# Two graph layers on one core: h M and h Wv^T by Strassen's scheme, half-size slots for adj and exp(a), interleaved weight loads, more slots for the last results

## The chip, the core and the metric

The kernel runs on one core of a Trainium2 chip, in fp32 throughout. TensorE (PE) multiplies, VectorE (DVE) adds and reduces, ScalarE (ACT) applies functions and copies, GpSimd (POOL) computes one power per tile and issues stores, SyncE (SP) issues loads. The metric is the device time of one execution in microseconds; the runs' median is given beside the one profiled execution.

## The reference

x is 3327 x 512, adj 3327 x 3327 with a full diagonal, all weights 512 x 512:

```python
h = relu(layernorm(x))
q, k, v = h @ Wq.T + bq, h @ Wk.T + bk, h @ Wv.T + bv
a = q @ k.T / sqrt(512) + adj + adj
x = x + softmax(a) @ v
h = relu(layernorm(x))
A2 = adj + I;  d = diag(A2) ** -0.5
temp = A2 @ h @ W.T
x = x + relu((d[:, None] * A2 * d[None, :]) @ temp)
```

## The kernel before

Rows are padded to 3328 = 26 tiles of 128 (`HALF` = 13 tiles each half). Matrix products are cut into 2 x 2 blocks and done by a scheme of seven block products instead of eight (Strassen's in Winograd's form): some sums of blocks are made on DVE first, and results are put together from shared partial results. A matmul's cost on PE depends on the width of its moving operand, 512 at most, one PSUM bank.

Since q k^T = h Wq^T Wk h^T plus terms, the kernel first makes M = Wq^T Wk and the vector u = Wk^T bq; keys are then h itself, and queries are q' = (h M + u) * scale. The stages, in order of program text:

1. **M and u** (L218-237). Wq's four blocks of rows, then Wk's four, then four x tiles and bv are loaded on SP's queue in that order; 16 matmuls make M, 16 narrow ones u.
2. **Layernorm and projections** (L184-296). A tile of x is loaded into one of four slots of `x_ring` (L192), `norm` (L168) takes its statistics on DVE and the power on POOL, ACT applies the relu in place, PE transposes four 128 x 128 pieces, ACT copies them to the block's `hb` and to `hp[t]`. `hp[t]` holds seven combinations of h's 2 x 2 blocks for key tile t, four of them made by DVE adds (L262-265); they are the scores' left operands. A block is 2 to 4 tiles; `h_transposed(b + 1)` stands ahead of `project(b)`. `project` makes q' transposed, four output blocks by four contraction blocks, moving width 512, 384 or 256, stored by POOL to `qd`; then v, four matmuls of width 512 a tile, stored to `vd`.
3. **Scores** (L303-406), 4 groups of query columns (two 448 wide, two 384 wide in each of four quarters) by 13 steps t. For a step, `adjacency` loads four quarter blocks of adj transposed into one slot of `g_ring` (4 slots, L304); `outer_sums` makes the four sums that the graph layer will need (`four_sums`, L149) in one of two `o` slots and stores them; `scores` does seven products of two matmuls. A bank Y is read by `plus` (L358) after each of the products 0-0, 4-5 and 2-7 and then accumulated onto, so that one product's value goes into several results. The last product is put off into the next step (`rest`, L377). ACT takes exp of g's halves (L373, L381/383), and one store writes all of g to `pd` (L384). Half a group ahead, `queries` loads four blocks of q' and `more_queries` makes four differences (L155).
4. **Attention** (L409-519). exp(a) is read back, `values` reads v and makes its differences, seven products a step of width 256, summed over 13 steps in seven banks; `attend` puts the results together in `cx`, divides by the row sums (L488), stores the new x and the new h.
5. **Graph layer** (L548-802). Two rounds g of the same recursion one level deeper: `Step` loads blocks of adj or their stored sums into `a_ring`, makes `four_sums` into `o_ring3`, `Right` makes the right operand's blocks in `b_ring`, `gather` puts the products together in `cts`. `temp` (L713) multiplies by W, `finish` (L723) transposes a result tile back, scales, adds x, and stores it from one of three slots of `out_ring` (L569). The last six half tiles are finished after the last step (L801).

On-chip memory is one `arena` with tags `big`, `half`, `quarter` (L95-102): a new tile under a tag waits until everything that used the tag's last tile is done. The order on each engine is made by a scheduler from the program text; the DMA queues of SP and POOL issue in order, so that an issue that waits for a slot holds those behind it.

Of the kernel before, what the change touches and what calls it, by code (L numbers as in the profile page):

```python
# [44 lines left out]
def graph_layers_kernel(  # L45
# [45 lines left out]

    arena = ctx.enter_context(tc.tile_pool(name="arena", bufs=1))
    banks = ctx.enter_context(tc.tile_pool(name="banks", bufs=1, space=bass.MemoryType.PSUM))

    def big(k, shape, name):  # L95
        return arena.tile(shape, F32, name=name, tag=f"big{k}")
# [44 lines left out]
    qd = [dram.tile([P, DC, 2 * H[s]], F32, name=f"qd{s}") for s in range(2)]  # L141
    vd = [dram.tile([P, D], F32, name=f"vd{i}") for i in range(NT)]
# [41 lines left out]
    hp = [big(t, [P, 7, 2, P], f"hp{t}") for t in range(HALF)]  # L184

    blocks = []
    for s in range(2):
        for a, z in ((0, 4), (4, HT[s])):
            for y in range(2):
                blocks.append((s, [STRIPS[s] + y * HT[s] + k for k in range(a, z)]))  # L190

    x_ring = ring((big, 13), (big, 14), (big, 15), (big, 16))  # L192
    v_ring = ring((big, 17), (big, 18), (quarter, 0))
    hb_ring = ring((half, 4), (half, 5), (half, 8), (half, 9), (half, 2), (half, 3))
    qs_ring = ring((half, 6), (half, 7), (half, 10), (half, 11))
# [4 lines left out]
    mm_ring, tp_ring, av_ring = psum_ring(0, 1, 2, 3), psum_ring(4, 5), psum_ring(6, 7)  # L200

    def load_x(i):
        xt = x_ring([P, D], "xt")
        nc.sync.dma_start(xt, x[i * P : (i + 1) * P])
        return xt

    def weight(name, src, slots):

        parts = []
        for k in range(2):  # L210
            w = half(slots[k], [P, 2, D], name)
            for c in range(2):
                r = (2 * k + c) * P
                nc.sync.dma_start(w[:, c], src[r : r + P])
            parts += [w[:, 0], w[:, 1]]
        return parts

    w_q = weight("wq", wq, (12, 13))  # L218
    w_k = weight("wk", wk, (0, 1))
    first = {i: load_x(i) for i in blocks[0][1]}  # L220
    bv_sb = quarter(1, [P, D], "bv_sb")
    nc.sync.dma_start(bv_sb, bass.AP(tensor=bv.tensor, offset=bv.offset, ap=[[0, P], [1, D]]))
    M = [m[:, c] for m in (half(14, [P, 2, D], "M"), half(15, [P, 2, D], "M")) for c in range(2)]
    u = const.tile([P, DC], F32, name="u")

    ps = [mm_ring("mm") for _ in range(DC)]
    for c in range(DC):
        for r in range(DC):
            nc.tensor.matmul(ps[r], w_q[c][:, r * P : (r + 1) * P], w_k[c], start=c == 0, stop=c == DC - 1)  # L229
    for r in range(DC):  # L230
        nc.scalar.copy(M[r], ps[r])
    pu = tp_ring("pu")
    for r in range(DC):
        for c in range(DC):
            nc.tensor.matmul(pu[:, r : r + 1], w_k[c][:, r * P : (r + 1) * P], bq_sb[:, c : c + 1],
                             start=c == 0, stop=c == DC - 1)
    nc.vector.tensor_copy(u, pu[:, :DC])

    w_v = weight("wv", wvT, (12, 13))

    hT = {}

    def h_transposed(b):

        _, its = blocks[b]
        hb = [hb_ring([P, 2, BW], "hb") for _ in range(2)]
        for k, i in enumerate(its):
            xt = first.pop(i) if i in first else load_x(i)
            rstd, nb = norm(xt)
            nc.scalar.activation(xt, xt, AF.Relu, bias=nb, scale=rstd)  # L250
            pt = tp_ring("tp").rearrange("p (c e) -> p c e", c=DC)
            for c in range(DC):
                nc.tensor.transpose(pt[:, c], xt[:, c * P : (c + 1) * P], ident)  # L253
            own = [a[:, :, k * P : (k + 1) * P] for a in hb]
            for a in range(2):
                nc.scalar.copy(own[a], pt[:, 2 * a : 2 * a + 2])
            t = i % HALF
            if i < HALF:
                nc.scalar.copy(hp[t][:, 0:2], pt.rearrange("p (a c) e -> p a c e", a=2))
            else:  # L260
                nc.scalar.copy(hp[t][:, 2], pt[:, 2:4])
                nc.vector.tensor_add(hp[t][:, 3], own[0], hp[t][:, 2])  # L262
                nc.vector.tensor_add(hp[t][:, 5], own[0], hp[t][:, 0])
                nc.vector.tensor_add(hp[t][:, 4], hp[t][:, 3], hp[t][:, 0])
                nc.vector.tensor_add(hp[t][:, 6], hp[t][:, 1], hp[t][:, 4])
        hT[b] = [hb[c // 2][:, c % 2] for c in range(DC)]

    def project(b):
        s, its = blocks[b]
        wd = len(its) * P  # L270
        hb = hT.pop(b)
        c0 = (its[0] - STRIPS[s]) * P
        for a in range(2):
            qs = qs_ring([P, 2, BW], "qs")
            for o in range(2):
                ps = mm_ring("mm")
                d = 2 * a + o
                for c in range(DC):
                    nc.tensor.matmul(ps[:, :wd], M[c][:, d * P : (d + 1) * P], hb[c][:, :wd],  # L279
# [900 lines left out]
```

## Time and profile before

| | us |
|---|---|
| median of 3 runs | 2306.88 (2306.67 to 2311.48) |
| profiled execution, its own time | 2312.0 |
| its span | 2310.2 |
| PE busy | 2250.0 (97%) |
| DVE busy | 1402.6 (61%) |
| ACT, POOL busy | 221.7, 208.5 |
| M and u, to | 27.1 |
| layernorm and projections, to | 218.6 |
| scores, to about | 757 |
| attention, to | 1276 |
| graph layer, to | 2283 |
| end | 2310.2 |

The profiled execution took 5.1 us more than the median. Shares of busy time are means over stages; a row such as `A <- B: total, times, longest` in the table of waits says how long A's engine stood before A until B was done. A timeline row gives start, length, engine, line, operation, output and inputs, shape, count, and in brackets the idle time before it and what ended it. DMA rows give the time from issue to landing.

### The profile page before, as it was taken

What the parts mean: (1) busy time and instruction counts of PE and PEld (TensorE: products, weight loads), DVE (VectorE), ACT (ScalarE), POOL (GpSimd) and SP (SyncE); (2) the same over time, 40 slices, a digit from 0 to 9 for tenths busy, and PEclk for the clock granted to TensorE, in tenths of its full rate; (3) what the DMA queues carried; (4) which work ended last, traced back from release to release, by engine and by line L of the source; (5) the groups of instructions that cost most, each with busy time, mean ns of one, the idle gap of its engine ahead of it and who ended that gap; (6) DMA issues with size and microseconds to landing.
All of it is one profiled execution on the core that took longest, in us unless ns stands there. A gap on an engine that the chain in (4) does not pass through costs nothing.

```text
span 2310.2 us, 21423 instructions
## 1 busy us (share of the span) xinstructions
PE 2250.0 (97%) x7398; PEld 1379.1 (60%) x7398; DVE 1402.6 (61%) x2845; ACT 221.7 (10%) x336; POOL 208.5 (9%) x332
## 2 busy tenths in 40 slices
PE   8999999999999999999999999999999999999995
PEld 4545444455555788888888555555545455555553
DVE  3344656666556765565655667787645357677773
ACT  3210111121111000000000000000001000000011
POOL 2121111111111010010110100000000000000001
PEclk9999999999999999999999999999999999999998
DMA  4334778777787443444445667766545467666684
GB/s 150 126 123 167 257 260 282 249 265 256 269 278 263 133 150 92 133 138 132 137 135 190 217 211 256 233 208 211 190 147 193 151 211 257 227 200 213 205 273 135
DMA packets 226086, 457.55 MB, mean 198 GB/s; under 512 B 23250, under 2 KB 129072, under 8 KB 225968
## 3 DMA queue, kind: packets, MB, share of 16 engines
q1 hardware_dynamic: 192464, 323.17, 43.8%
q0 software_dynamic: 33504, 132.92, 15.6%
q8 instruction: 60, 0.98, 0.2%
q14 instruction: 58, 0.48, 0.1%
HBM read 323.11 MB, written 132.90 MB: 197 GB/s over the span
## 4 chain that ended last, share of the span: by engine, by line
PE 62%; issue 29%; POOL 4%; DMA 2%; DVE 2%; ACT 0%; SPq 0%; POOLq 0%; DVEq 0%
PE p L660 28%; PE p L516 22%; PE p L718 4%; PE p L652 3%; PE av L287 2%; PE mm L279 2%; POOL sum L346 1%; POOL p L384 1%; PE mm L229 1%; POOL out_dram L88 1%; DMA p<-g 1%; DMA g<-in_adjT_dram 1%; PE tp L253 0%; POOL rstd L177 0%; DVE st L171 0%
## 5 line engine op out<-in xcount | busy, mean ns | idle before, releaser
L660 PE MATMUL p<-o,b 128*128 128x448 f32 (+1 forms) x1344 | 526.8, 514 | 0.0
L660 PE MATMUL p<-a,b 128*128 128x448 f32 (+1 forms) x1008 | 418.1, 513 | 3.7 <-DVE b L623 3.7
L660 PEld LDWEIGHTS p<-o,b 128*128 128x128 f32 x1344 | 255.6, 190 | 213.6 <-issue 120.0
L355 PE MATMUL Y<-qt,hp 128*128 128x448 f32 (+1 forms) x832 | 314.0, 520 | 19.3 <-DVE g L359 19.2
L516 PE MATMUL p<-vr,o 128*128 128x256 f32 x1352 | 322.0, 379 | 2.7 <-DVE vr L157 2.2
L151 DVE TENSOR_TENSOR o<-a 128x896 f32<-128x896 f32 (+1 forms) x168 | 171.8, 1022 | 215.9 <-PE p L660 183.4
L660 PEld LDWEIGHTS p<-a,b 128*128 128x128 f32 x1008 | 189.9, 190 | 161.9 <-issue 91.6
L516 PEld LDWEIGHTS p<-vr,o 128*128 128x128 f32 x1352 | 256.5, 190 | 38.9 <-DVE vr L157 2.6
L355 PEld LDWEIGHTS Y<-qt,hp 128*128 128x128 f32 x832 | 157.1, 191 | 162.0 <-issue 73.3
L516 PE MATMUL p<-vr,pt 128*128 128x256 f32 x1014 | 250.2, 379 | 0.0
L516 PEld LDWEIGHTS p<-vr,pt 128*128 128x128 f32 x1014 | 192.2, 190 | 26.3
L355 PE MATMUL Z<-qt,hp 128*128 128x448 f32 (+1 forms) x416 | 162.4, 513 | 0.0
L509 DVE TENSOR_TENSOR sums<-sums,pt 128x512 f32<-128x512 f32 (+1 forms) x84 | 54.7, 651 | 148.5 <-DMA pt<-p 148.4
L359 DVE SCALAR_TENSOR_TENSOR g<-g,Y 128x448 f32<-128x448 f32 (+1 forms) x156 | 91.1, 584 | 70.0 <-PE Y L355 67.8
L355 PEld LDWEIGHTS Z<-qt,hp 128*128 128x128 f32 x416 | 79.3, 191 | 66.7 <-issue 39.4
L151 DVE TENSOR_TENSOR o<-g 128x896 f32<-128x896 f32 (+1 forms) x52 | 53.2, 1024 | 101.7 <-DMA g<-in_adjT_dram 97.0
L152 DVE TENSOR_TENSOR o<-o,a 128x448 f32<-128x448 f32 (+1 forms) x168 | 98.8, 588 | 3.8
L153 DVE TENSOR_TENSOR o<-o,a 128x448 f32<-128x448 f32 (+1 forms) x168 | 98.8, 588 | 3.4
L718 PE MATMUL p<-w,ct 128*128 128x512 f32 x208 | 93.5, 592 | 0.0
L279 PE MATMUL mm<-hb,M 128*128 128x512 f32 (+2 forms) x256 | 92.0, 512 | 0.0
L287 PE MATMUL av<-wv,hb 128*128 128x512 f32 x208 | 91.2, 593 | 0.0
L652 PE MATMUL p<-a,b 128*128 128x448 f32 (+1 forms) x224 | 82.8, 513 | 0.0
(140 smaller groups left out, 1790.2 us busy)
## 6 DMA issues: line engine op xcount, KB each, us to landing
a<-sum SPq DMA_DIRECT2D x104, 448.0 KB, 5.6
pt<-p SPq DMA_DIRECT2D x78, 512.0 KB, 4.2
a<-sum SPq DMA_DIRECT2D x104, 384.0 KB, 3.7
a<-in_adjT_dram SPq DMA_DIRECT2D x78, 448.0 KB, 4.4
a<-in_adjT_dram SPq DMA_DIRECT2D x78, 384.0 KB, 3.7
g<-in_adjT_dram SPq DMA_DIRECT2D x52, 448.0 KB, 5.7
sum<-o POOLq DMA_DIRECT2D x26, 896.0 KB, 5.5
p<-g POOLq DMA_DIRECT2D x26, 896.0 KB, 4.3
```

Of the source, the lines that this page charges most:

```text
L151: nc.vector.tensor_add(o[:, 0:2], g[:, 0:4:3], g[:, 1:2].to_broadcast([P, 2, g.shape[-1]]))
L152: nc.vector.tensor_add(o[:, 2], o[:, 1], g[:, 0])
L153: nc.vector.tensor_add(o[:, 3], o[:, 2], g[:, 2])
L279: nc.tensor.matmul(ps[:, :wd], M[c][:, d * P : (d + 1) * P], hb[c][:, :wd], start=c == 0, stop=c == DC - 1)
L287: nc.tensor.matmul(ps, hb[c][:, k * P : (k + 1) * P], w_v[c], start=c == 0, stop=c == DC - 1)
L355: nc.tensor.matmul(ps, hp[t][:, a, k], qt[b][:, k], start=start and k == 0, stop=k == 1, skip_group_check=True)
L359: nc.vector.scalar_tensor_tensor(g[:, n], g[:, n], 2.0, ps, op0=ALU.mult, op1=op)
L509: nc.vector.tensor_add(sums, sums, pt[:, 0:2])
L516: nc.tensor.matmul(ps[r][:, m * E : (m + 1) * E], a[:, m * P : (m + 1) * P], vr[t][:, b], start=t == 0 and m == 0, stop=t == HALF - 1, ski ...
L652: nc.tensor.matmul(ps[("p2", "p3", "p4", "p8")[k]][:, :w], b[:, z], a[:, 0, y], start=k == 3, stop=True)
L660: nc.tensor.matmul(ps[r][:, :w], b[:, i], m, start=self.t == 0, stop=self.t == PAIRS - 1 and r in ("p1", "p5", "p6", "p7"))
L718: nc.tensor.matmul(ps, cts[s][d][:, k * P : (k + 1) * P], w1[d], start=d == 0, stop=d == DC - 1)
```

## The change

- **Layernorm and projections.** Tiles are taken in four packs of 3, 3, 3 and 4 tiles from each half, both halves together (6 or 8 tiles). The pack's `hp` holds the seven combinations, and these are now also the left operands of seven-product schemes for q' = h M + u and v = h Wv^T + bv; M and Wv get `four_differences` and a negated first block. `hb` is gone. A class `Chain` holds the order of products and reads that the scores had, and serves q', v and the scores; the last product of a chain is put off into the next chain.
- **Start.** Blocks of Wq and Wk are loaded in turns; the first four x tiles are issued on ACT's queue; Wv has slots of its own and is loaded in halves of a block.
- **Scores.** `g` is split into halves by tile row, with rings of 4 and 5 half-size slots; `o` is split into two of four half-size slots; each half of exp(a) and of the sums is stored by itself, the first half of exp(a) as soon as it is ready.
- **Attention, graph layer.** `cx`, s1, u, v, q and `cts` are smaller tiles; normalization of a tile is done in two halves; the graph layer's rings are views of the packs' space; the first half of the last gather is settled before the last adds of the second.
- **End.** The last six half tiles have six slots for results and six for x.

The diff, cut; where a function is rewritten, only its new lines are given:

```diff
-    def big(k, shape, name):
-        return arena.tile(shape, F32, name=name, tag=f"big{k}")
+    def large(k, shape, name):
+        return arena.tile(shape, F32, name=name, tag=f"large{k}")
+    def mid(k, shape, name):
+        return arena.tile(shape, F32, name=name, tag=f"mid{k}")
...
-    qd = [dram.tile([P, DC, 2 * H[s]], F32, name=f"qd{s}") for s in range(2)]
-    vd = [dram.tile([P, D], F32, name=f"vd{i}") for i in range(NT)]
+    qd = dram.tile([P, DC, NP], F32, name="qd")
+    vd = [dram.tile([P, 4, E], F32, name=f"vd{t}") for t in range(HALF)]
...
+    PACKS = ((0, 3), (3, 3), (6, 3), (9, 4))
+    A = {"m1": 0, "p2": 1, "p4": 2, "p5": 3, "p6": 4, "p7": 5, "p3": 6}
+    B = {"m1": 0, "p2": 2, "p3": 3, "p5": 4, "p6": 5, "p7": 6, "p4": 7}
+    hp = [large(k, [P, 7, 2, n * P], f"hp{k}") for k, (_, n) in enumerate(PACKS)]
+    def h_of(t, product, c):
+        k = next(k for k, (a, n) in enumerate(PACKS) if a <= t < a + n)
+        o = (t - PACKS[k][0]) * P
+        return hp[k][:, A[product], c, o : o + P]
...
+    x_bank, y_bank, z_bank, tp_bank = psum_ring(0, 1), psum_ring(2, 3), psum_ring(4, 5), psum_ring(6, 7)
+    class Chain:
+        before = None
+        def __init__(self, product, first, more, last):
+            X, Y, Z = x_bank("X"), y_bank("Y"), z_bank("Z")
+            product(Y, "m1", True)
+            first(0, Y, -1)
+            product(Z, "p5", True)
+            first(3, Z, -1)
+            product(X, "p2", True)
+            more(0, X)
+            product(Y, "p6", False)
+            first(1, Y, -1)
+            Chain.finish()
+            product(Z, "p3", False)
+            more(1, Z)
+            product(Y, "p7", False)
+            more(3, Y)
+            def rest():
+                product(Y, "p4", False)
+                first(2, Y, 1)
+                last()
+            Chain.before = rest
+        @staticmethod
+        def finish():
+            if Chain.before:
+                Chain.before()
+            Chain.before = None
+    x_ring = ring(*((mid, k) for k in range(4)))
+    v_ring = ring(*((mid, k) for k in range(5, 13)))
+    def load_x(i, queue=nc.sync):
         xt = x_ring([P, D], "xt")
+        queue.dma_start(xt, x[i * P : (i + 1) * P])
...
+    order = [(k, t + y * HALF) for k, (a, n) in enumerate(PACKS) for t in range(a, a + n) for y in range(2)]
+    first = {i: load_x(i, nc.scalar) for _, i in order[:4]}
+    def blocks(slots, name):
+        return [b[:, k] for b in (half(j, [P, 2, 2, E], name) for j in slots) for k in range(2)]
+    w_q, w_k = ([half(k, [P, 2, D], name) for k in slots] for name, slots in (("wq", (0, 1)), ("wk", (2, 3))))
+    for c in range(DC):
+        for w, src in ((w_q, wq), (w_k, wk)):
+            nc.sync.dma_start(w[c // 2][:, c % 2], src[c * P : (c + 1) * P])
+    bv_sb = quarter(0, [P, D], "bv_sb")
     nc.sync.dma_start(bv_sb, bass.AP(tensor=bv.tensor, offset=bv.offset, ap=[[0, P], [1, D]]))
+    w_v = blocks(range(8, 12), "wv")
+    for c in range(DC):
+        for z in range(2):
+            nc.sync.dma_start(w_v[2 * (c // 2) + z][:, c % 2], wvT[c * P : (c + 1) * P, z * E : (z + 1) * E])
+    M = blocks(range(4, 8), "M")
...
+            nc.tensor.matmul(ps[r], w_q[c // 2][:, c % 2, r * P : (r + 1) * P], w_k[c // 2][:, c % 2],
+                             start=c == 0, stop=c == DC - 1)
     for r in range(DC):
+        for z in range(2):
+            nc.scalar.mul(M[2 * (r // 2) + z][:, r % 2], ps[r][:, z * E : (z + 1) * E], scale)
+    pu = bank(4, "pu")
     for r in range(DC):
         for c in range(DC):
+            nc.tensor.matmul(pu[:, r : r + 1], w_k[c // 2][:, c % 2, r * P : (r + 1) * P], bq_sb[:, c : c + 1],
                              start=c == 0, stop=c == DC - 1)
+    nc.vector.tensor_scalar(u, pu[:, :DC], scale, None, op0=ALU.mult)
+    for b in (M, w_v):
+        four_differences(b)
+        nc.scalar.mul(b[0], b[0], -1.0)
...
+    def h_transposed(k):
+        a, n = PACKS[k]
+        for _, i in (o for o in order if o[0] == k):
             xt = first.pop(i) if i in first else load_x(i)
             rstd, nb = norm(xt)
...
+            w = slice((i % HALF - a) * P, (i % HALF - a + 1) * P)
             if i < HALF:
+                nc.scalar.copy(hp[k][:, 0:2, :, w], pt.rearrange("p (a c) e -> p a c e", a=2))
             else:
+                nc.scalar.copy(hp[k][:, 2, :, w], pt[:, 2:4])
+                nc.vector.tensor_add(hp[k][:, 3, :, w], hp[k][:, 2, :, w], pt[:, 0:2])
+                nc.vector.tensor_add(hp[k][:, 5, :, w], hp[k][:, 0, :, w], pt[:, 0:2])
+        nc.vector.tensor_add(hp[k][:, 4], hp[k][:, 3], hp[k][:, 0])
+        nc.vector.tensor_add(hp[k][:, 6], hp[k][:, 1], hp[k][:, 4])
+    def project_q(k):
+        a, n = PACKS[k]
+        w = n * P
+        qs = [half(12 + j, [P, 2, BW], "qs") for j in range(4)]
+        def chain(o):
+            def product(ps, name, start):
+                for c in range(2):
+                    nc.tensor.matmul(ps[:, :w], M[B[name]][:, c, o * P : (o + 1) * P], hp[k][:, A[name], c],
+                                     start=start and c == 0, stop=c == 1, skip_group_check=True)
+            def first(j, ps, sign):
+                d = 2 * (j % 2) + o
+                nc.scalar.activation(qs[j][:, o, :w], ps[:, :w], AF.Identity, bias=u[:, d : d + 1], scale=float(sign))
+            def more(j, ps):
+                nc.vector.tensor_add(qs[j][:, o, :w], qs[j][:, o, :w], ps[:, :w])
+            def last():
+                if o == 1:
+                    for j in range(4):
+                        y, z = divmod(j, 2)
+                        i = (y * HALF + a) * P
+                        nc.gpsimd.dma_start(qd[:, 2 * z : 2 * z + 2, i : i + w], qs[j][:, :, :w])
+            Chain(product, first, more, last)
+        for o in range(2):
+            chain(o)
+    def project_v(k):
+        a, n = PACKS[k]
+        def chain(t0, m):
+            vs = [v_ring([P, 2, E], "vs")[:, :m] for _ in range(4)]
+            def product(ps, name, start):
+                for j in range(m):
+                    for c in range(2):
+                        nc.tensor.matmul(ps[:, j * E : (j + 1) * E], h_of(t0 + j, name, c), w_v[B[name]][:, c],
+                                         start=start and c == 0 and j == 0, stop=c == 1, skip_group_check=True)
+            def of(ps):
+                return ps[:, : m * E].rearrange("p (j e) -> p j e", j=m)
+            def first(j, ps, sign):
+                z = j % 2
+                bias = bv_sb[:, z * E : (z + 1) * E].unsqueeze(1).to_broadcast([P, m, E])
+                (nc.vector.tensor_add if sign > 0 else nc.vector.tensor_sub)(vs[j], bias, of(ps))
+            def more(j, ps):
+                nc.vector.tensor_add(vs[j], vs[j], of(ps))
+            def last():
+                for j in range(m):
+                    for y in range(4):
+                        nc.gpsimd.dma_start(vd[t0 + j][:, y], vs[y][:, j])
+            Chain(product, first, more, last)
+        for t0 in range(a, a + n, 2):
+            chain(t0, min(2, a + n - t0))
...
+        project_q(k)
+        project_v(k)
...
-    g_ring = ring(*((big, k) for k in range(13, 17)))
-    o_ring = ring((big, 17), (big, 18))
-    x_bank, y_bank, z_bank = psum_ring(0, 1), psum_ring(2, 3), psum_ring(4, 5)
+    g_rings = ring(*((mid, k) for k in range(4))), ring(*((mid, k) for k in range(4, 9)))
+    o_ring = ring(*((mid, k) for k in range(9, 13)))
...
-        g = g_ring([P, 4, Q[0]], "g")[:, :, :wd]
+        g = [take([P, 2, Q[0]], f"g{k}")[:, :, :wd] for k, take in enumerate(g_rings)]
         for k in range(2):
             r0, c0 = (k * HALF + t) * P, STRIPS[s] * P
             src = adjT[r0 : r0 + P, c0 : c0 + 2 * H[s]].rearrange("p (y w) -> p y w", y=2)
-            nc.sync.dma_start(g[:, 2 * k : 2 * k + 2], src[:, :, c : c + wd])
+            nc.sync.dma_start(g[k], src[:, :, c : c + wd])
...
-        o = o_ring([P, 4, Q[0]], "o")[:, :, :wd]
-        four_sums(o, g)
+        pair = [o_ring([P, 2, Q[0]], "o")[:, :, :wd] for _ in range(2)]
+        o = [pair[m // 2][:, m % 2] for m in range(4)]
+        nc.vector.tensor_add(o[0], g[0][:, 0], g[0][:, 1])
+        nc.vector.tensor_add(o[1], g[1][:, 1], g[0][:, 1])
+        nc.vector.tensor_add(o[2], o[1], g[0][:, 0])
+        nc.vector.tensor_add(o[3], o[2], g[1][:, 0])
         for n, parts in enumerate(((0, 2, 3), (0, 1, 2, 3), (3,), (1, 2, 3))):
             k, y = divmod(n, 2)
-            d = diagonal(o[:, 0], (k * HALF + t) * P, STRIPS[s] * P + y * H[s] + c)
+            d = diagonal(o[0], (k * HALF + t) * P, STRIPS[s] * P + y * H[s] + c)
             for m in parts if d else ():
-                nc.vector.tensor_add(o[:, m, d[0]], o[:, m, d[0]], d[1])
-        nc.gpsimd.dma_start(sumd[s][t][:, :, c : c + wd], o)
+                nc.vector.tensor_add(o[m][:, d[0]], o[m][:, d[0]], d[1])
+        for m in range(2):
+            nc.gpsimd.dma_start(sumd[s][t][:, 2 * m : 2 * m + 2, c : c + wd], pair[m])
+    def scores(s, q, t, qt, g):
         wd, c = Q[s], q * Q[s]
+        a = [g[0][:, 0], g[0][:, 1], g[1][:, 0], g[1][:, 1]]
+        def product(ps, name, start):
             for k in range(2):
+                nc.tensor.matmul(ps[:, :wd], h_of(t, name, k), qt[B[name]][:, k], start=start and k == 0, stop=k == 1,
                                  skip_group_check=True)
+        def settle(k):
+            if k == 1 and t == HALF - 1:
+                nc.scalar.activation(g[k], g[k], AF.Exp, bias=pad)
             else:
+                nc.scalar.activation(g[k], g[k], AF.Exp)
+            nc.gpsimd.dma_start(pd[s][t][:, 2 * k : 2 * k + 2, c : c + wd], g[k])
+        def first(n, ps, sign):
+            nc.vector.scalar_tensor_tensor(a[n], a[n], 2.0, ps[:, :wd], op0=ALU.mult,
+                                           op1=ALU.add if sign > 0 else ALU.subtract)
+        def more(n, ps):
+            nc.vector.tensor_add(a[n], a[n], ps[:, :wd])
+            if n == 1:
+                settle(0)
+        Chain(product, first, more, lambda: settle(1))
...
-    sum_ring = ring((half, 14), (half, 15))
+    sum_ring = ring((half, 7), (half, 14))
-    b12_ring = ring((big, 15), (big, 16), (big, 17), (big, 18))
+    b12_ring = ring(*((mid, k) for k in range(4, 8)))
...
+        nc.sync.dma_start(vr[t][:, 0], vd[t][:, 0])
+        nc.sync.dma_start(b12, vd[t][:, 1])
+        nc.sync.dma_start(vr[t][:, 1:3], vd[t][:, 2:4])
...
-            nc.vector.scalar_tensor_tensor(xt, cx[y][:, k], rs, xt, op0=ALU.mult, op1=ALU.add)
+            for z in range(2):
+                w = slice(z * E, (z + 1) * E)
+                nc.vector.scalar_tensor_tensor(xt[:, w], cx[y][z][:, k], rs, xt[:, w], op0=ALU.mult, op1=ALU.add)
...
+    def view(k, j):
+        if k not in parts:
+            n = PACKS[k][1]
+            parts[k] = large(k, [P, n, 4, Q[0]], f"part{k}")
+        return parts[k][:, j]
+    def turns(*views):
+        turn = itertools.cycle(views)
+        return lambda: view(*next(turn))
+    a_ring = turns((0, 0), (0, 1), (0, 2), (1, 0), (1, 1))
+    o_ring3 = turns((1, 2), (2, 0), (2, 1))
...
+    spare = ((mid, 10), (mid, 11), (mid, 12))
     ts_ring = ring((quarter, 0), (quarter, 1), (half, 8))
-    xr_ring = ring((quarter, 0), (quarter, 1), (half, 8))
-    out_ring = ring((half, 6), (half, 14), (half, 9))
+    xr_ring = ring((quarter, 0), (quarter, 1), (half, 8), (half, 9))
+    out_ring = ring((half, 6), (half, 7), *spare[:2])
+    xr_last = ring(*((half, k) for k in (15, 14, 10, 11, 8, 9)))
+    out_last = ring((half, 6), (half, 7), *spare, (quarter, 0))
...
+        if r == "p4" and s == 1:
+            settle(lo)
         nc.vector.tensor_add(to[0][:, hi], v, p["p4"])
         nc.vector.tensor_add(to[1][:, hi], to[1][:, hi], p["p8"])
         if r == "p4" and s == 1:
-            settle(lo)
             settle(hi)
...
-        xr = xr_ring([P, D], "xr")
+        xr = (xr_ring if spot is None else xr_last)([P, D], "xr")
-        pt = bank(spot, "pt")
+        pt = bank(ROLE["p8"] if spot is None else spot, "pt")
+            nc.tensor.transpose(pt[:, d * P : (d + 1) * P], cts[s][y][d][:, k * P : (k + 1) * P], ident)
+        o = (out_ring if spot is None else out_last)([P, D], "r")
```

## The prediction

> **What bounds the kernel now.** I read the page's busy shares first (PE 97%, DVE 61%, ACT 10%), then a table of windows cut at the stage borders, because a 97% mean hides where the other 3% and the cheaper work lie.
>
> ```profile
> 7.75:27.10 19.35, 19.35 (x64) 10.41 (x65) 3.96 (x17) 6.77 (x9) 6.69 (x5) 1.00 0.48 139
> 27.10:218.60 191.50, 191.10 (x570) 98.53 (x570) 80.16 (x202) 43.33 (x101) 37.71 (x63) 1.00 0.39 133
> 218.60:495.00 276.40, 269.78 (x713) 134.38 (x712) 176.36 (x321) 48.45 (x51) 36.92 (x52) 1.00 0.74 257
> 495.00:757.70 262.70, 250.05 (x753) 142.74 (x752) 162.34 (x325) 46.77 (x55) 37.01 (x52) 0.99 0.78 268
> 757.70:1276.00 518.30, 515.57 (x2411) 453.40 (x2409) 311.56 (x698) 22.18 (x30) 41.41 (x67) 1.00 0.44 136
> 1276.00:2283.00 1007.00, 1002.06 (x2885) 538.36 (x2884) 662.84 (x1268) 51.67 (x84) 43.95 (x79) 1.00 0.64 212
> 2283.00:2310.20 27.20, 2.10 (x13) 1.24 (x12) 5.03 (x12) 2.52 (x6) 3.98 (x8) 0.60 0.18 61
> ```
>
> Columns: window and length, then PE, weight load, DVE, ACT, POOL, then granted clock, DMA share, GB/s. Rows: M and u; layernorm and projections; the scores' first two and last two groups; attention; the graph layer; the tail. PE is the bound everywhere except the tail; the scores leave it idle for some 19 us, which no other stage does. Next, the PE timeline for what a matmul costs by width (each fp32 matmul is two records; next start minus start, over the count, is the real rate, since ends are modelled):
>
> ```profile
> 74.12 13.90 PE L287 MATMUL av<-wv,hb 128*128 128x512 f32 x32
> 87.86 1.04 PE L253 MATMUL tp<-ident,xt 128*128 128x128 f32 x8
> ...
> 90.46 9.20 PE L279 MATMUL mm<-hb,M 128*128 128x384 f32 x28
> 99.49 5.74 PE L287 MATMUL av<-wv,hb 128*128 128x512 f32 x13
> ...
> 308.45 3.17 PE L355 MATMUL Y<-qt,hp 128*128 128x448 f32 x8
> 311.45 1.67 PE L355 MATMUL Z<-qt,hp 128*128 128x448 f32 x4
> ...
> 788.46 1.89 PE L516 MATMUL p<-vr,pt 128*128 128x256 f32 x8
> 790.18 2.75 PE L516 MATMUL p<-vr,o 128*128 128x256 f32 x12
> ```
>
> 512 wide: 13.74/32 = 0.429 us a record; 384: 9.03/28 = 0.3225; 448: 3.00/8 = 0.375; 256: 1.72/8 = 0.215. Cost follows width, so fewer products is less time. Then the waits, and the rows around a stall:
>
> ```profile
> PE Y L355 <- DVE g L359: 19.2, 22, 2.4
> DVE o L151 <- DMA g<-in_adjT_dram: 97.0, 42, 4.1
> ```
> ```profile
> 625.69 0.96 DVE L151 TENSOR_TENSOR o<-g 128x768 f32<-128x768 f32 x1 [2.95 <-DMA g<-in_adjT_dram]
> ...
> 524.71 2.85 PE L355 MATMUL Y<-qt,hp 128*128 128x384 f32 x8 [1.49 <-DVE g L359]
> ...
> 629.36 4.54 PE L355 MATMUL Y<-qt,hp 128*128 128x384 f32 x8 [2.21 <-DVE g L359]
> ```
>
> DVE stands at the adj sums of a step two ahead, for a load whose ring slot came free late; behind them on DVE is the add that reads PE's bank Y; so PE stands too. The last pair shows a second price: after 1.49 us idle, eight records cost 2.85 us; after 2.21 us they cost 4.54, at a granted clock of 0.88 there. A long stall costs its length plus 1.7 us. The tail:
>
> ```profile
> 2291.33 0.47 ACT L734 ACTIVATE r<-pt,sd 128x256 f32<-128x256 f32 x1 [4.97 <-DMA out_dram<-r]
> ```
>
> The sum is made against the profiled execution, 2312.0 us (span 2310.2); the runs' median, 2306.88, is 5.1 below it, and is what the sum is lastly compared with.
>
> **Stage 1, matmuls.** Before: q' 128x0.429 + 64x0.3225 + 64x0.215 = 89.3, v 208x0.429 = 89.2, transposes 104x0.13 = 13.5; 192.0 in all, and the window has 191.5, so this stage is matmul rate alone. After, seven products for eight: q' 168x0.3225 (packs of 3) + 56x0.429 (pack of 4) = 78.2, v 364x0.215 = 78.3, transposes as before: 170.0. **-22.0.** What it adds on other engines (v's seven adds a chain for one a tile, four differences of M and of Wv, 52 stores of v for 26, at 0.55 us an issue on POOL) lies beside PE: DVE would go from 80 us to about 110 and POOL from 38 to about 52 of 170. Without that cover POOL's 26 extra issues would cost 14 us.
>
> **Start.** Wq and Wk blocks now alternate, and the first x loads leave SP for ACT's queue. PE's first matmul waited 7.7 us for the first Wk block, fifth in its queue (issued at 3.06, landed at 7.61); it is now second (about 1.6), but shares the engines with x (229 GB/s moved in that window: 1.5 MB are 6.5 us). -1.0, bounds 0 and -1.5.
>
> **A new hole at the first pack.** Before, four x tiles, as many as the ring's slots, made the first block, and PE ran on after the four transposes. Now pack 0 is six tiles and the x ring still has four slots: tiles five and six are loaded once transposes free slots. Rows of before: second x load issued 27.82, its bn_stats at 30.40 (2.6 later), its relu 33.37 to 34.18, transposes 0.5, ACT's copy 0.6. In the new order PE has M and u done at 26.1 and frees the first slot at 26.7; 26.7 + 2.6 + 4.5 (statistics, with two adds of h and a second tile's statistics ahead of them on DVE) + 0.8 + 0.5 + 0.6 puts the first product at about 36. PE has 3.1 us of transposes to do from 26.1: about 6.9 idle, and 1.7 for the restart by the 2.21 us row. **+8.7**, bounds 6 (statistics as quick as in the rows) and 10.
>
> The Trainium skill ("TensorE: Matmul & The Clock Gate", "Why this matters for your kernels") allows idle gaps up to about 3 us before the clock falls. The 2.21 us row disagrees with it; by the page this hole, cut by transposes, might cost no restart, and the sum would be 1.7 lower.
>
> **Waits inside the new chains.** 16 chains each return three times to a bank that DVE or ACT must have read: 48 waits. The nearest row is the same pattern in the scores: 22 waits in 19.2 us, but of some 150 such returns, and those for DVE's late loads. Two products (1.7 to 2.6 us) stand between, against adds of 0.4 to 0.7. Bounds 1 and 42 (48x0.87, each like one of the 22); near the low end, because DVE and ACT here wait for few loads: **+4**.
>
> **Stage 1 to 2.** The first group's queries now need the last pack's q, and g and o slots are v's. Rows: a q' store 3.2 to landing, a query load 4.1; the g loads and PE's v of the last pack (112x0.215 = 24 us) cover them. +1.5, bounds 0 and 4.
>
> **Scores.** Matmul rate alone: 728x0.375 + 728x0.3225 = 507.8; taken from 218.6 to about 756: 537.5. So 29.7 us are lost, most in the 384-wide half (262.7 against 234.8). The ring cycle now: last add, exp, store issued (0.7), 4.3 to land, load issued, 5.7 or 4.8 to land, the sums: with hops 12.9 us, against a step of 10.5 or 9.0. With halves: the first half's exp comes about 1.5 us earlier, its store is half as large (a 256 KB store took 2.3, a 512 KB one 3.2: some 3.1), and its load no longer stands behind the other half's: 9.7 to 10.9 against some 9.8 needed (448) and 9.5 against 8.5 (384). DVE then waits 0 to 2 us, and the rows show that PE bears about 2 us of DVE's waiting. DVE pays four sums for three (0.15 us a step), two more issues on POOL (1.3 us): both have room (64% and 13% busy in that window). **-20**, bounds -8 and -27. The matmuls are the same.
>
> **Attention, graph layer.** Same matmuls, same order on PE but for a few swaps; windows of 518.3 and 1007.0 are at matmul rate (515.6 and 1002.1 busy). The last store of p is half as long: -0.5. The split normalization (26 x 0.15 us on DVE, 60% busy) is hidden; with no cover it would be 4. New views of the freed packs' space: no slot's waits change. 0.
>
> **Tail.** Three finish slots for six results: the fourth waited 4.97 us for a store to land. Six slots end that, and the half settled one matmul role earlier is already under PE's last work. **-5**, bounds -4.5 and -5.5.
>
> **Sum.** -22.0 - 1.0 + 8.7 + 4 + 1.5 - 20 - 0.5 - 5 = -34.3; 2312.0 - 34.3 = 2277.7, so 2278. From the median instead it would be 2272.6; I keep the higher, since waits I did not find are likelier than gains.
>
> **Rivals.**
> - *A, as summed*: 2278; own range 2266 to 2290 from the bounds. 0.60.
> - *B, the halves don't shorten the loop* (the change doesn't do what it says): the new order puts the adj sums three steps ahead rather than two, so DVE still stands for loads; the DMA share of 0.78 says transfers slow one another. For A: loads land in 5 us alone as well as there. Scores -2: 2312 - 16 = 2296; 2290 to 2302. 0.14.
> - *C, the hole closes and all stalls go*: hole +6, chains +1, scores -27: 2312 - 49.5 = about 2262. Against: the 384-wide chain is a microsecond longer than its step. 0.12.
> - *D, slower: stage 1's waits*. Each of the 48 returns costs what one cost in the scores, 0.87 us: 42 rather than 4, so 2278 + 38 = 2316. It decides from 29/48 = 0.6 us each (2306.9 - 2277.7 = 29). For it: ACT now stands in the chain (q's first reads), in order behind relus that wait for x. Against: two products between write and return. 0.14.
>
> A range to leave out 2 in 10 runs from 2262 to 2300 (A, C's upper half, B). Measurement tells 0.2%, 4.6 us, from no change; A, B and C are all beyond it on the fast side, less a little of B: faster 0.84, same 0.03, slower 0.13.
>
> **What would show it.** Window of stage 1: PE busy about 170 with the stage 183 to 187 long, and one idle of 2 us or more on transposes at 29 to 36. Few rows "PE Y <- DVE" over 1 us in the scores, stage 515 to 520 long, clock 1.00. Last ACT read with no wait for a store. Attention and graph layer within 2 us of 518 and 1007. Wrong if the scores' length stays over 530, if PE waits repeatedly for ACT in stage 1, or if the graph layer's loads wait for slots.

## The result

The changed kernel took 2361.19 us (2358.74 to 2367.09), against 2307.48 for the kernel before: 1.0233 times, interval 1.0210 to 1.0256. The forecast was 2278 with a range of 2262 to 2300. The profiled execution, the longest of the four, took 2367.1 us; its span is 2365.2.

First the table of windows of the changed kernel, cut at its own stage borders (columns as above: window, length, busy time of PE, weight load, DVE, ACT, POOL, then granted clock, DMA share, GB/s):

```profile
8.00:26.50 18.50, 18.50 (x52) 8.98 (x51) 5.65 (x18) 6.61 (x14) 6.11 (x4) 1.00 0.57 162
26.50:205.00 178.50, 172.50 (x696) 124.23 (x696) 87.11 (x207) 47.45 (x81) 48.73 (x84) 0.96 0.43 138
205.00:810.00 605.00, 536.43 (x1452) 281.09 (x1451) 342.26 (x693) 93.62 (x104) 151.81 (x211) 0.96 0.69 231
810.00:1330.00 520.00, 516.56 (x2396) 452.07 (x2395) 312.30 (x719) 23.82 (x31) 39.35 (x69) 1.00 0.44 138
1330.00:2337.00 1007.00, 1003.15 (x2900) 541.42 (x2899) 662.27 (x1270) 50.99 (x83) 41.83 (x76) 1.00 0.67 213
```

The loss is in one row. The scores' window of 605 us holds 536 us of PE at a clock of 0.96; before, two windows of together 539 us held 520. Attention and graph layer have the lengths they had. DMA share and GB/s went down in the scores (0.69 and 231, from 0.74 to 0.78 and 257 to 268), so the transfers did not fill up; they waited.

Since the last projections and the first scores are interleaved, I counted each stage from its own matmul records (from first to last, less what the other stage's records took in between; PE's wait at the border to the scores, 4.2 us in the changed kernel, is counted to the projections):

| stage, us | before | changed | difference | in the sum |
|---|---|---|---|---|
| start, to the first transpose | 27.1 | 28.5 | +1.4 | -1.0 |
| layernorm and projections | 191.3 | 183.0 | -8.3 | -9.3 with +1.5 at the border |
| scores | 537.8 | 603.8 | +66.0 | -20 |
| attention | 519.5 | 521.9 | +2.4 | -0.5 |
| graph layer | 1007.5 | 1006.2 | -1.3 | 0 |
| last matmul to end | 27.1 | 21.7 | -5.3 | -5 |
| span | 2310.2 | 2365.2 | +55.0 | -34.3 |

(-9.3 is -22.0 + 8.7 + 4.) All rows but one came out within 3 us of the sum, the projections in part by luck (see below); the scores missed by 86.

The table of waits (waiting engine and its operation, what it waited for: total, times, longest) names the place:

```profile
DVE o L423 <- DMA g<-in_adjT_dram: 159.2, 46, 6.0
PE Y L441 <- DVE g L452: 68.3, 39, 4.4
...
SPq L416 <- DMA p<-g: 479.6, 95, 14.1
```

Before, these were 97.0 us in 42 times, 19.2 in 22, and 365.5 in 48. L423 is the first of the four adj sums, L452 the add that reads PE's bank, L416 the load of half of g, and what that load waits for is the store of half of exp(a), `p<-g`. One step of the timeline, 448 wide (rows picked in order of time):

```profile
418.08 0.62 DVE L423 TENSOR_TENSOR o<-g 128x448 f32<-128x448 f32 x1 [2.87 <-DMA g<-in_adjT_dram]
418.62 0.62 DVE L424 TENSOR_TENSOR o<-g,g 128x448 f32<-128x448 f32 x1
419.16 0.61 DVE L456 TENSOR_TENSOR g<-g,Z 128x448 f32<-128x448 f32 x1
...
419.85 0.95 ACT L448 ACTIVATE g<-g 128x896 f32<-128x896 f32 x1 [3.66 <-DVE g L456]
...
420.82 0.72 POOL L433 DMA_DIRECT2D sum<-o  x1 [2.26 <-DVE o L431]
...
421.55 0.73 POOL L449 DMA_DIRECT2D p<-g  x1
...
427.44 0.37 SPq L416 DMA_DIRECT2D g<-in_adjT_dram  x1
...
431.30 0.62 DVE L423 TENSOR_TENSOR o<-g 128x448 f32<-128x448 f32 x1 [4.79 <-DMA g<-in_adjT_dram]
...
432.37 0.61 DVE L456 TENSOR_TENSOR g<-g,Z 128x448 f32<-128x448 f32 x1
...
435.30 3.27 PE L441 MATMUL Y<-qt,hp 128*128 128x448 f32 x8 [1.94 <-DVE g L452]
```

This is a closed circle. The sums of step k+3 (L423, L424) stand on DVE ahead of the add of Z for step k (L456). That add lets exp of step k's first half start; its store frees the slot into which the first half for step k+4 is loaded; and the sums of step k+4 stand ahead of the next add of Z. From 418.08 once round to 431.30 are 13.2 us: two sums 1.08, add and exp to 420.81, the store issued at 421.55 behind a store of sums on POOL, landed at 427.38, load landed at 431.20. The matmuls of a step need 28 x 0.375 = 10.5. Over 21 such steps the means are 1.08 + 1.65 (median) + 0.30 (median) + 4.26 (store) + 0.05 + 4.36 (load) = 11.7, and a step took 12.2; over 25 steps 384 wide, where 9.0 are needed, 10.9 and 11.1.

### The profile page after: what moved, and what is told of

Same layout as the page of the kernel before. It is cut to its first block, busy times and chain, and to the rows that moved or that the text cites. A ratio compares the mean times of both kernels' runs of the same rounds, so it can differ in the third digit from the quotient of the medians.

```text
span 2365.2 us, 22424 instructions
## 1 busy us (share of the span) xinstructions
PE 2256.0 (95%) x7522; PEld 1413.1 (60%) x7522; DVE 1420.9 (60%) x2935; ACT 227.7 (10%) x322; POOL 294.6 (12%) x462
## 4 chain that ended last, share of the span: by engine, by line
PE 59%; issue 28%; POOL 6%; DMA 4%; DVE 2%; ACT 0%; POOLq 0%; SPq 0%; DVEq 0%; ACTq 0%
PE p L768 27%; PE p L593 17%; PE p L827 4%; POOL sum L433 3%; PE p L760 2%; POOL p L449 2%; PE Y L352 2%; PE Y L321 2%; PE Z L352 1%; PE Z L321 1%; DMA p<-g 1%; DMA g<-in_adjT_dram 1%; PE mm L277 1%; POOL out_dram L88 1%; PE tp L301 0%
## 5 line engine op out<-in xcount | busy, mean ns | idle before, releaser
L768 PE MATMUL p<-part,b 128*128 128x448 f32 (+1 forms) x2352 | 835.4, 513 | 2.4 <-DVE b L731 1.6
L768 PEld LDWEIGHTS p<-part,b 128*128 128x128 f32 x2352 | 445.4, 190 | 374.1 <-issue 210.0
L441 PE MATMUL Y<-qt,hp 128*128 128x448 f32 (+1 forms) x832 | 330.9, 539 | 68.6 <-DVE g L452 68.3
L155 DVE TENSOR_TENSOR part<-part 128x896 f32<-128x896 f32 (+1 forms) x168 | 171.9, 1024 | 164.4 <-PE p L768 104.9
L448 ACT ACTIVATE g<-g 128x896 f32<-128x896 f32 (+1 forms) x100 | 89.6, 896 | 467.5 <-DVE g L452 327.2
L452 DVE SCALAR_TENSOR_TENSOR g<-g,Y 128x448 f32<-128x448 f32 (+1 forms) x156 | 91.2, 585 | 64.0 <-PE Y L441 62.9
L423 DVE TENSOR_TENSOR o<-g 128x448 f32<-128x448 f32 (+1 forms) x52 | 30.8, 592 | 163.8 <-DMA g<-in_adjT_dram 159.2
L449 POOL DMA_DIRECT2D p<-g x104 | 75.4, 725 | 290.1 <-ACT g L448 272.1
L433 POOL DMA_DIRECT2D sum<-o x104 | 75.4, 726 | 170.4 <-DVE o L424 123.7
L157 DVE TENSOR_TENSOR part<-part,part 128x384 f32<-128x384 f32 (+1 forms) x146 | 86.1, 590 | 8.9 <-DVE part L156 0.5
L156 DVE TENSOR_TENSOR part<-part,part 128x384 f32<-128x384 f32 (+1 forms) x146 | 86.1, 590 | 3.1
L760 PE MATMUL p<-part,b 128*128 128x448 f32 (+1 forms) x224 | 82.8, 513 | 0.0
L441 PE MATMUL X<-qt,hp 128*128 128x448 f32 (+1 forms) x208 | 81.1, 513 | 0.0
```

The lines of the kernel that those rows point to most:

```text
L155: nc.vector.tensor_add(o[:, 0:2], g[:, 0:4:3], g[:, 1:2].to_broadcast([P, 2, g.shape[-1]]))
L156: nc.vector.tensor_add(o[:, 2], o[:, 1], g[:, 0])
L157: nc.vector.tensor_add(o[:, 3], o[:, 2], g[:, 2])
L433: nc.gpsimd.dma_start(sumd[s][t][:, 2 * m : 2 * m + 2, c : c + wd], pair[m])
L441: nc.tensor.matmul(ps[:, :wd], h_of(t, name, k), qt[B[name]][:, k], start=start and k == 0, stop=k == 1, skip_group_check=True)
L448: nc.scalar.activation(g[k], g[k], AF.Exp)
```

## The experiments

The kernel before was run beside each; the medians of those runs were 2307.4 to 2309.1. The changed kernel was not run again beside them; its 2361.19 us are those of the result. A number such as "0.9876 of before" is the ratio to the runs of before beside it, with its 95% interval.

**The order on DVE alone.** Theory 1 is that circle; theory 2 is that more and smaller transfers are late wherever the sums stand. An ordering edge moves the sums and takes no wait, slot or transfer away:

```diff
-        outer_sums(*groups[n], t, g)
+        if k >= 2:
+            with tc.issue_after(z_adds[k - 2]):
+                outer_sums(*groups[n], t, g)
```

(`z_adds` collects the adds of Z, step by step; DVE may take up the sums of step k only after the add of step k-2.)

> The changed kernel, with one ordering edge added: on DVE the four adj sums of step j may stand only behind the Z add of step j-2 (the add that completes the first half of exp(a)). Now they stand three steps ahead, in front of the Z add of step j-3. Theory 1 (a loop): the sums of step k+3 wait for a load whose slot is freed by the store of exp of step k-1, and the add that lets exp of step k start is queued behind those sums, so each step lasts the loop's 12 to 13 us (add, exp, store, load, sums) instead of the matmuls' 10.5 or 9.0. With the edge the sums have a whole step more: waits of PE for DVE in the scores fall from 68 us to under 10, the scores from some 609 us to 515 to 525, the time to about 2270. Theory 2 (twice as many stores and issues of half the size make the transfers themselves late, wherever the sums stand): the edge changes little, 2345 or more.

2279.36 us (2277.26 to 2283.82), 0.9876 of before (0.9853 to 0.9899): 82 us less than the changed kernel. Its waits and the window of its scores:

```profile
PE Y L441 <- DVE g L452: 9.3, 4, 4.2
```
```profile
202.00:728.00 526.00, 516.71 (x1468) 280.42 (x1467) 349.98 (x697) 95.19 (x106) 153.26 (x213) 0.99 0.79 268
```

DVE's wait for g is gone, the scores take 519.1 us, and the same stores and loads now move 268 GB/s. The longest of PE's four waits, 4.2 us, is that at the border. Theory 2 falls.

**One place later.** The edge goes to the Z add of step j-3: the sums still reach three steps ahead, but stand behind the add instead of in front of it.

> The changed kernel, with the four adj sums of step j behind the Z add of step j-3: one place later on DVE than now, lookahead the same. Theory 1: the loop stays closed but is shorter by the two sums (about 1.1 us) that stood ahead of the Z add: some 11 us a step against 10.5 and 9.0, so the scores take about 575 and the time is 2325 (2305 to 2340). Theory 2: 2345 or more, as without the edge.

2285.19 us (2281.21 to 2290.49), 0.9894 (0.9866 to 0.9922), scores 527.0. Both theories missed: I had expected a circle shorter by 1.1 us, and more than the whole loss went. The waits:

```profile
DVE o L423 <- DMA g<-in_adjT_dram: 27.1, 22, 3.9
PE Y L441 <- DVE g L452: 15.8, 9, 4.7
```

DVE still stands for loads 22 times, but step k's add now stands ahead of the sums of step k+3, so a late load for step k+3 no longer holds up the store that makes room for the load of step k+4. The order itself, not the length of the chain, was the loss: slots and lookahead are the changed kernel's, store and load together take 9.0 us in the mean against 8.6 there (448 wide), and 76 us are gone.

**Half-size slots alone, in the kernel before.** `g_ring` and `o_ring` become rings of halves (4, 5 and 4 slots), with four separate sums and a store for each half; projections, weights and tail stay.

```diff
-        g = g_ring([P, 4, Q[0]], "g")[:, :, :wd]
+        g = [take()[:, :, :wd] for take in g_rings]
...
-            nc.gpsimd.dma_start(pd[s][t][:, :, c : c + wd], g)
+            nc.gpsimd.dma_start(pd[s][t][:, 2 * k : 2 * k + 2, c : c + wd], g[k])
```

> The kernel before with one part of the change alone: g and o in half-size slots (rings of 4, 5 and 4), four separate sums, a store for each half of exp(a) and of the sums. Theory 1: the sums move three steps ahead, in front of the Z add, and the loop closes as in the changed kernel: scores from 538 to 590 to 610, time 2355 to 2380. Theory 3 (the loss comes from the rest of the change, such as packs of h, v's slots and the chain that runs on from the projections): 2285 to 2310.

2361.47 us (2354.18 to 2366.51), 1.0232 (1.0208 to 1.0257): as long as the changed kernel, from this part alone, and theory 3 falls. The scores take 588.4 us, 50.6 more than before; the 15 us by which the changed kernel's scores are longer still (603.8) come with the rest of the change, and their cause stays open. The waits:

```profile
DVE whole L354 <- DMA whole<-in_adjT_dram: 150.0, 47, 5.7
PE Y L373 <- DVE whole L379: 51.3, 35, 3.5
```

(`whole` is the tile that the halves lie in). The order of DVE's adds is what these kernels differ in; S22 is the first of the sums of step 22, X20 and Z20 are two adds of step 20 ("full slots, with an edge" is a run shown below):

```
before                    X20 S22 Z20      two steps ahead
changed, halves alone     X20 S23 Z20      three steps ahead, ahead of the add
edge of the second run    X20 Z20 S23      three steps ahead, behind the add
edge of the first run     X20 Z20 S22
full slots, with an edge  X20 Z20 S21
```

With full slots, a slot comes free only after the second half's exp, whose add stands on DVE ahead of the sums; so before, as I read it, a late load stopped DVE and PE, but not its own successor. What counts, by these orders, is how many steps one turn of the circle reaches over. In the changed kernel and with halves alone it is one: S23 holds up Z20, and Z20's store makes room for the load of S24. Before, and with the second run's edge, it is two: in the second run S23 holds up Z21, which makes room for S25; before, S22 holds up the last add of step 20, which makes room for S24. With the first run's edge, and with full slots and an edge, it is three, so that a turn has three steps' time. PE's waits for DVE in the scores go the same way: 68 us in the changed kernel and 57 with halves alone; 19 before and 16 in the second run; 9 in the first run and 2 with full slots and an edge (some 4 us of the 68, the 16 and the 9 lie at the border). That the scheduler moves the sums up because a half slot is free sooner is what the listings suggest; it was not tried by itself.

**Halves alone, with the edge; full slots, with an edge.** The kernel with half-size slots alone (the fourth run on record) gets the edge of the first run; and the kernel before gets

```diff
-        outer_sums(*groups[n], t, g)
+        if k >= 1:
+            with tc.issue_after(z_adds[k - 1]):
+                outer_sums(*groups[n], t, g)
```

> The kernel before with half-size slots alone (as in the fourth run) and the edge of the first run. Theory 1: the loop opens here too, scores from 589 us to 512 to 520, time 2283 to 2290. Theory 2 (the number of transfers costs by itself): 2300 or more.

> The kernel before, full-size slots, with the sums of step j held behind the Z add of step j-1 (before: two steps ahead, in front of it). If the stalls of before come from where the sums stand and not from the size of the slots, the scores fall from 538 to 512 to 520 us and the time to 2283 to 2290, without halves. If slots of full size come free too late wherever the sums stand: 2300 to 2309.

2284.99 us (2282.03 to 2287.14), 0.9904 (0.9887 to 0.9920), and 2282.89 (2282.27 to 2284.53), 0.9893 (0.9878 to 0.9908); scores 513.9 and 510.6. So 27 of the 29.7 us that the scores lost before could be had by the place of the adj sums in DVE's order, and half-size slots are worth nothing here: at the right order, full ones do as well. The window of the scores with full slots and the edge, and what PE still waited for in it:

```profile
220.00:733.00 513.00, 510.64 (x1463) 277.34 (x1462) 340.21 (x632) 95.29 (x106) 73.86 (x104) 1.00 0.80 276
```
```profile
PE Y L355 <- DVE g L359: 1.2, 1, 1.2
PE Y L355 <- DVE g L375: 1.1, 1, 1.1
```

**The hole at the first pack.** Six x slots instead of four, all six loaded at the start:

```diff
-    x_ring = ring(*((mid, k) for k in range(4)))
+    x_ring = ring(*((mid, k) for k in range(5)), (quarter, 1))
-    first = {i: load_x(i, nc.scalar) for _, i in order[:4]}
+    first = {i: load_x(i, nc.scalar) for _, i in order[:6]}
```

> The changed kernel with six x slots instead of four and all six tiles of the first pack loaded at the start on ACT's queue. Prediction's hole: PE's idle of 4.6 us ahead of the fifth tile's transposes and the slow records after it go, 5 to 8 us less, about 2355. Rival (the hole is regained later, because the scores are bound by their transfers and not by when they start): within 2 us of the changed kernel's 2361.

2350.0 us (2349.6 to 2355.17), 1.0183 of before (1.0158 to 1.0207), 11 less than the changed kernel. The hole was there; PE's rows of the changed kernel:

```profile
31.77 1.09 PE L301 MATMUL tp<-ident,xt 128*128 128x128 f32 x4 [0.40 <-DVE hp L308]
37.41 1.97 PE L301 MATMUL tp<-ident,xt 128*128 128x128 f32 x8 [4.56 <-ACT xt L298]
39.21 2.37 PE L321 MATMUL Y<-hp,M 128*128 128x384 f32 x4
```

4.56 us idle, and then four records of 384 in 2.20 us where four take 1.29. With six slots the projections take 178.5 us, 4.5 less. The other 6.7 us lie mostly in the scores (596.4 against 603.8), whose circle turned a little faster; why is not settled. So the gain is more than the hole explains.

**The border to the scores.** The sums' four slots are the last that v's results leave. The slots of g's second half and of the sums are exchanged, on top of the first run's edge:

```diff
-    g_rings = ring(*((mid, k) for k in range(4))), ring(*((mid, k) for k in range(4, 9)))
-    o_ring = ring(*((mid, k) for k in range(9, 13)))
+    g_rings = ring(*((mid, k) for k in range(4))), ring(*((mid, k) for k in (4, 9, 10, 11, 12)))
+    o_ring = ring(*((mid, k) for k in range(5, 9)))
```

> The edge of the first run, and the slots of g's second half and of the sums exchanged: in the changed kernel the sums' four slots are those that the last v results leave last (DVE stands at the third sum of a step until v's store has landed, and PE 4.2 us with slow records after it, at the border from projections to scores). If that slot is the cause, the 4.2 us and the restart go: 2274 (2271 to 2277). Rival (the first group's query and adj loads arrive no earlier, so another wait takes its place): 2277 to 2281.

2267.72 us (2265.74 to 2269.78), 0.9828 (0.9813 to 0.9843), 11.6 less than the first run, more than twice what I expected. In the changed kernel DVE had stood at the third sum for a store of v, and PE behind it:

```profile
213.11 0.62 DVE L425 TENSOR_TENSOR o<-o,g 128x448 f32<-128x448 f32 x1 [3.14 <-DMA vd<-vs]
215.39 3.23 PE L441 MATMUL Y<-qt,hp 128*128 128x448 f32 x4 [4.21 <-DVE g L452]
218.46 1.03 PE L352 MATMUL Y<-wv,hp 128*128 128x256 f32 x4
```

and with the exchanged slots:

```profile
209.75 1.77 PE L441 MATMUL Y<-qt,hp 128*128 128x448 f32 x4 [1.34 <-DVE g L452]
211.36 1.89 PE L352 MATMUL Y<-wv,hp 128*128 128x256 f32 x8
```

PE's wait fell by 2.9 us and the slow records behind it by 1.5. What is left has another cause: DVE now waits 3.07 us at the second sum, for the load of g's second half, into a slot that v had. In the profiles, whose spans differ by 9.2 us, the projections' stage is 4.4 us shorter than in the first run, the scores' 4.2 and the attention 3; start and graph layer are 2.4 longer. In the attention the first run shows a wait of PE of 1.93 us, and then a granted clock of 0.50 from 740.0 to 743.4; this run has a wait of 1.59 there and no such stretch. Of the difference of the medians, 1.6 us lie between the runs of before in the two comparisons (2309.1 and 2307.5).

**All three together.**

> The changed kernel with all three: the edge two steps behind, the exchanged slots, six x slots. If the three terms add: 2279 - 5 - 5 to 11 = 2263 to 2270. If the earlier end of the projections is lost again at the border: 2272 or more.

2265.49 us (2263.51 to 2268.37), 0.9820 (0.9806 to 0.9833): faster than both kernels, 42 us less than before. Of the six x slots, 2.2 us are left in the median, and the two kernels' runs overlap, though the projections' stage is 5.7 us shorter than in the run before it (173.0 against 178.7).

**The last slots alone, in the kernel before.**

```diff
+    out_last = ring(*((half, k) for k in (6, 14, 9, 7, 15, 10)))
...
+        o = (out_ring if spot is None else out_last)([P, D], "r")
```

> The kernel before with one part of the change alone: six slots for the results of the last six half tiles (x still comes into three). The prediction's term: no wait of 5.0 us for a store before the fourth result, time 4.5 to 5.5 lower, 2301 to 2303. Rival (the end is set by the landing of the last stores, whichever slot they come from, or by x's three slots): within 2 us of before.

2306.17 us, 0.9987 (0.9975 to 1.0000): 1.2 us, not 5. ACT no longer waits for a store; DVE waits for x in its place:

```profile
2281.42 2.30 ACT L735 ACTIVATE r<-pt,sd 128x256 f32<-128x256 f32 x6 [3.87 <-PE pt L733]
2284.50 0.42 DVE L736 TENSOR_TENSOR r<-r,xr 128x256 f32<-128x256 f32 x1 [1.43 <-DMA xr<-x1d]
2286.76 0.42 DVE L736 TENSOR_TENSOR r<-r,xr 128x256 f32<-128x256 f32 x1 [1.83 <-DMA xr<-x1d]
```

x for the last results came into three slots. The change has six for these too.

## Why the prediction was wrong

- **What failed: the scores' term, "-20, bounds -8 and -27".** It measured +66. The step of the prediction that failed is "DVE then waits 0 to 2 us, and the rows show that PE bears about 2 us of DVE's waiting". The rows that showed this are of a kernel in which the wait delayed nothing that it itself waited for later. I took over the tolerance without asking what stands behind the sums on DVE. I had the new order in hand (rival B says that the sums move three steps ahead) and priced it at no gain, -2. The question that gives the answer is: does the awaited load's next turn depend on an instruction queued behind the waiting one? If so, and if one turn reaches over one step alone, the chain's length is the step's length and no slack helps. In its place the runs showed DVE waiting 159.2 us in 46 times and PE behind it 64 us in the scores, with steps of 12.2 and 11.1 us for matmuls of 10.5 and 9.0; the half-size slots alone bring the loss, and moving the sums behind one add takes it away.
- **The chain's size** was off too, but by less: 9.7 to 10.9 us forecast, 11.7 measured (448). The half store took 4.26 us from issue, where I had 3.1 from stores of the projections, a stage with a DMA share of 0.39. With the true chain and the circle, the sum is (11.7 - 10.5) x 26 + (10.9 - 9.0) x 26 = 81 us above matmul rate, 588 in all. Measured were 603.8, since the steps took 12.2 and 11.1, a little more than the means of the chain's parts.
- **Rival B**'s mechanism (the new order undoes the gain) was the nearest, but its price did not allow a loss; **rival D** put the slow side into the projections' 48 returns. These cost nothing that the profile shows: no row has PE waiting inside the chains of q' and v; stage 1 has waits of PE for the hole, the border and about 1.4 us at transposes besides. There was no rival in which the scores themselves became slower.
- **Strassen for q' and v**: -9.3 forecast and -8.3 measured agree in part by luck. The 22 us less of matmuls hold. But the hole cost 4.5 to 5.7 us (by the runs with six x slots) where the sum had 8.7, and the waits inside the chains nothing where it had 4; instead 5.8 us at the border, for which the sum had 1.5, and 1.4 at transposes lie in this row. With hole and border wait gone the stage takes 173.0, 18.3 less than before.
- **The border**, +1.5 with bounds 0 and 4, was undersized: 4.2 us of wait and 1.6 of slow records in the changed kernel. I had covered the load of g and of the queries, but not the sums' slots, which wait for v's last stores.
- **The clock.** The 2.21 us row of before was the right guide for the size of a restart, but not for when it comes: after 4.56 us idle four records took 0.9 us too long, after 4.21 us 1.6 too long. From the border to the end of the scores the changed kernel's granted clock fell to 0.50 ten times, for 3.4 or 6.8 us, and its mean there was 0.96. PE stood 37 times for 0.5 us or more in that stretch. Each of the five stalls of 3.85 to 4.43 us had a fall beside it; of the 32 shorter ones five had (1.92 to 2.85 us), while others of 2.33 to 2.47 us had none. Two rows, the first at a granted clock of 1.00, the second running into 3.4 us at 0.50 that begin at 706.5:

```profile
284.30 1.77 PE L441 MATMUL Y<-qt,hp 128*128 128x448 f32 x4 [2.37 <-DVE g L452]
705.53 2.03 PE L441 MATMUL Y<-qt,hp 128*128 128x384 f32 x4 [1.92 <-DVE g L452]
```

The Trainium skill ("TensorE: Matmul & The Clock Gate", "Why this matters for your kernels") sets the limit at about 3 us of idle; the five falls after shorter stalls disagree with it. Records in the ten stretches took some 20 us more than at full rate, so the 96 us above matmul rate (603.8 against 507.8) are 64 of waits, some 20 of clock, and some 11 that I can't place.
- **The tail**, -5, measured -5.3 in the profiles, but not for the reason given alone, and the agreement is in part luck: results' slots by themselves gave 1.2 us. From the last matmul to the landing of the last store the changed kernel took 10.3 us against 13.3; the other 2.3 us lie after that landing, where the change does nothing.
- **Attention and graph layer**: -0.5 and 0 forecast, +2.4 and -1.3 measured. At the start of the attention PE waits some 2 us in both kernels (2.22 before, 2.17 in the changed one); in the changed one the granted clock is then 0.50 from 829.4 to 832.8, in the kernel before it stays at 1.00.
- **The start**, -1.0: the first Wk block was there at 7.6 us instead of 7.7, and u was done 1.4 us later. No gain shows; over the variants of both kernels the start varies between 25.1 and 28.5, more than the term.

## What to carry to other kernels

When a change lets buffers come free earlier, look at where the consumer of the next load then stands in its engine's order: if the instruction that frees the slot is queued behind the one that waits for it, the ring becomes a circle. Count how many steps one turn reaches over: where it is one, each step lasts as long as store, load and the adds between them together; at two or three, the same turn has two or three steps' time. That waits cost little before is no measure of what they cost in a circle of one step. Ask first whether the stall can be had by order alone: here one ordering edge gave 25 us where half-size buffers lost 52.

## What was not expected of the hardware

- The same stores and loads of 448 KB had other times in another order of DVE's adds: in the changed kernel's 448-wide steps the store of a first half took 4.26 us in the mean and the load that follows it 4.36, with the first run's edge 3.30 and 5.76. A sum of a store and a load, 8.6 and 9.1, moved less than either.
- From the landing of the last result to the end of the span, 13.6 to 13.8 us pass in the kernel before and its two variants with full slots, 11.4 to 11.9 in the changed kernel and its five variants, and 9.5 in the two with halves alone. It goes with the program, and what sets it stays open.
